# q rows read three half groups late, two short-lived PSUM tiles, a longer ring: one change to a sparse attention layer

## The chip, the cores and the metric

The kernel runs on one core of a Trainium2 chip. The metric is the device time of one execution in microseconds. The engines are named as the profile names them: PE is TensorE (PEld its weight loads), DVE is VectorE, ACT is ScalarE, POOL is GpSimd, SP is SyncE. Each engine runs its own queue of instructions in a fixed order. The order is fixed when the program is built, and an instruction that has to wait holds up everything behind it in its queue.

## The reference, cut to what matters

One layer of graph attention over 4096 nodes with 512 features and 8 heads of 64. A node attends only where the adjacency matrix has an edge. The matrix is sparse: a node has about 17 edges on average, itself included, and none has more than 39 here.

```python
hs = layer_norm(x, ln1_scale, ln1_bias)            # sources
ht = layer_norm(h_target, ln1_scale, ln1_bias)     # targets
q = (ht @ Wq + bq).reshape(T, H, HD) / sqrt(HD)
k = (hs @ Wk + bk).reshape(S, H, HD)
v = (hs @ Wv + bv).reshape(S, H, HD)
logits = einsum('thd,shd->hts', q, k)
probs = softmax(where(adj != 0, logits, NEG))
ctx = einsum('hts,shd->thd', probs, v).reshape(T, D)
ht = layer_norm(ht + ctx @ Wo + bo, ln2_scale, ln2_bias)
y = ht + gelu(ht @ W1) @ W2                        # W1: 512 x 2048, W2: 2048 x 512
x = layernorm(x + y)
```

## The kernel before

The kernel never forms the 4096 x 4096 logits. It has three stages that overlap.

1. Keys and values of all nodes are computed and written to DRAM (`kvd`, one row of 1024 floats per node). Meanwhile the adjacency matrix is read, a list of neighbours is made for each node (`edges`), and the nodes are sorted by degree (`sort`). This is done in two parts of 2048 nodes, A and B. The lists of B are made while attention on A already runs.
2. Attention works on tiles of 128 targets of similar degree. A tile has room for `cap` edges per target, between 11 and 39. The edges are taken in groups of S = 3: for each edge GpSimd gathers one row of `kvd` per target into a slot of a ring.
3. The feed-forward part (`feed`) runs on TensorE between the attention steps, one or two tiles behind.

For one group of edges, attention does this (cut; "..." marks what is left out):

```python
nc.vector.tensor_tensor(kv[:, :n, :D], kv[:, :n, :D], tq[:, :D]..., ALU.mult)    # L1169: k * q
nc.vector.tensor_reduce(lg[:, :n, :], ..., AX.X, ALU.add)                         # L1173: logits
if j0 > 0:
    nc.scalar.activation(p[:, j0:j0 + n, :], lg[:, :n, :], AF.Exp)                # L1177
advance()                     # one step of every front and finish that is under way
yield cost * n
if pend:
    values(*pend.pop())       # the group before this one, see below
    issue(k + AHEAD)          # AHEAD = 4: gathers of the group four further on
advance()
if j0 == 0:
    p = ps.tile([P, MAXE, H], F32, name="p")                                      # in PSUM
    nc.scalar.activation(p[:, :n, :], lg[:, :n, :], AF.Exp)                       # L1187
if n == S:
    by_scalar(kv, lg)         # ScalarE scales the third edge's values, L1149 and L1152
```

The stretch between two calls of `advance` is a half group. `values` scales the values by `p` (VectorE, L1132); in part B it adds two of the three edges first (L1136). TensorE then adds them up, transposed, in PSUM (L1140):

```python
nc.vector.tensor_tensor(v4, v4, p..., ALU.mult)                                   # L1132
if m > 1 and i >= NA:
    nc.vector.tensor_add(kv[:, 0, D:], kv[:, 0, D:], kv[:, 1, D:])                # L1136
for j in slots:
    for c in range(KC):
        nc.tensor.matmul(cps[:, c, :], kv[:, j, ...], ident, is_transpose=True, ...)   # L1140
```

Two generators are stepped by `advance`: `front` makes the q rows of a tile before it starts, `finish` brings a tile to an end. Each `yield` is half a group.

```python
def front(i):
    tq = sp.tile([P, 2 * D], F32, name="tq", bufs=3)
    gather(t, h_target, rec[:, TGT:TGT + 1])
    yield
    nc.scalar.activation(t, t, AF.Identity, ...)                                  # L978
    yield
    pt = ps.tile([P, KC, P], F32, name="t")
    nc.tensor.transpose(pt[:, kc, :], ...)                                        # L982
    nc.scalar.activation(hT[:, kc, :], pt[:, kc, :], ...)                         # L985
    yield
    yield
    pq = ps.tile([P, D], F32, name="t")
    nc.tensor.matmul(pq, hT[:, kc, :], wq[:, kc, :], ...)                         # L991
    nc.vector.scalar_tensor_tensor(tq[:, :D], pq, HD ** -0.5, bqr, ...)           # L993: the q row
    tqs[i] = tq

def finish(i, p, cps, group, hs, mv):
    pm = sp.tile([P, MAXE, H], F32, name="pm", bufs=1)
    nc.vector.scalar_tensor_tensor(pm, rec, 0.0, p, op0=ALU.is_gt, op1=ALU.mult)  # L1037
    nc.vector.tensor_reduce(sums[:, i, :], pm..., AX.X, ALU.add)                  # L1040
    ...                                                                           # 1 / sum: ri
    nc.scalar.copy(rxf..., ri...)                                                 # L1047
    yield
    yield
    prx = ps.tile([P, KC, P], F32, name="t")
    nc.tensor.transpose(prx[:, c, :], rxf..., ident)                              # L1053
    ct = sp.tile([P, KC, P], F32, name="rb", bufs=1)
    nc.scalar.copy(ct, prx)                                                       # L1055
    yield
    nc.vector.tensor_mul(ct, cps, ct)                                             # L1057
    yield
    yield
    pa = ps.tile([P, D], F32, name="t")
    nc.tensor.matmul(pa[:, c * P:(c + 1) * P], tq..., ident, is_transpose=True)   # L1063
    nc.tensor.matmul(pa, ct[:, c, :], wo[:, c, :], ...)                           # L1067
    yield
    h = sp.tile([P, D], F32, name="h")
    nc.scalar.copy(h, pa)                                                         # L1071
    ...                                              # layer norm of h, ending in L1084
    pt = ps.tile([P, 2, 2 * P], F32, name="t")
    nc.tensor.transpose(pt..., h..., ident)                                       # L1093
    nc.scalar.activation(h2T[:, kc, :w], pt[:, k, :w], ...)                       # L1097
```

The pool `ps` has one buffer for each name unless it says otherwise. So every tile named `t`, whether `pt`, `pq`, `prx` or `pa`, takes the same PSUM bank, and a new one waits until the one before it has been read. `cps` has two banks and `p` one; four more belong to the projections, and later to the feed-forward: `pf` (L1277, emptied by the Gelu at L1280) and `po` (L1286).

The gathered rows lie in a ring of RING = 17 slots, `place` gives each group its slots. The adjacency blocks and masks that the lists of part B need have buffers of their own (`a`, two of 4 KB per partition; `sg`, three of 1 KB). At the end `verdict` sets a flag, which all engines load into a register. It decides whether a general path that takes any adjacency matrix has to run as well; with these inputs it does not.

Of the kernel before, what the change touches and what calls it, by code (L numbers as in the profile page):

```python
# [8 lines left out]
F32 = mybir.dt.float32  # L9
# [8 lines left out]
P = 128  # L18
# [425 lines left out]
def adj_resnorm_kernel(  # L444
# [59 lines left out]
    RING = 17  # L504
# [10 lines left out]
    flag = const.tile([1, 1], I32, name="flag")  # L515

# [13 lines left out]
    with tc.tile_pool(name="keep", bufs=1) as keep:  # L530
# [17 lines left out]
        with ExitStack() as late:  # L548
# [13 lines left out]

            ring = kp.tile([P, RING, 2 * D], F32, name="kv")

# [31 lines left out]
            def list_constants():  # L596
                io = lp.tile([P, QW], I32, name="a", bufs=2)
# [4 lines left out]
                io = lp.tile([P, QW], I32, name="a", bufs=2)  # L602
# [18 lines left out]
            pc = ps.tile([P, D], F32, name="t")  # L621
# [73 lines left out]
            def quarter(i, h):  # L695
                if i < NA + FILL:
                    a = ring[:, (i * NQ + h) % DEEP, :].bitcast(I32)
                else:
                    a = lp.tile([P, QW], I32, name="a", bufs=2)
                nc.sync.dma_start(a, adj[i * P:(i + 1) * P, h * QW:(h + 1) * QW])  # L700
                return a

            def edges(i):
# [4 lines left out]
                for h in range(NQ):  # L708
# [5 lines left out]
                    sg = lp.tile([P, QW], U8, name="sg", bufs=3)  # L714
# [13 lines left out]
                dec = lp.tile([P, 2, SEG, 8], U16, name="dec")  # L728
# [65 lines left out]
            def sort(part):  # L794
# [6 lines left out]
                dif = pool.tile([P, n], F32, name="dif")  # L801
# [5 lines left out]
                b16 = pool.tile([P, n], BF16, name="b16")  # L807
                nc.vector.tensor_scalar(b16, dif, -1.0, float(NB - 1), op0=ALU.mult, op1=ALU.add)
                if part:
                    oh = pool.tile([P, QW], I32, name="a", bufs=2).bitcast(BF16)  # L810
# [6 lines left out]
                pos = pool.tile([P, QW], I32, name="a", bufs=2).bitcast(F32)  # L817
# [4 lines left out]
                for c in range(2):  # L822
                    sl = slice(c * w, (c + 1) * w)
                    pt = ps.tile([P, w], F32, name="t")
# [5 lines left out]
                for c in range(2):  # L830
                    sl = slice(c * w, (c + 1) * w)
                    pa = ps.tile([P, w], F32, name="t")
# [3 lines left out]
                rank = pool.tile([P, n], F32, name="rank")  # L836
                nc.vector.tensor_reduce(rank, pos.rearrange("p b i -> p i b"), AX.X, ALU.add)
                ranki = pool.tile([P, n], I32, name="ranki")
# [14 lines left out]
            def project(order, t=None):  # L853
# [28 lines left out]
                def turn(n):  # L882
# [4 lines left out]
                    for k2 in range(KC // 2):  # L887
                        pt = (psi if k2 else ps).tile([P, 2, GR], F32, name="pt" if k2 else "t")
# [80 lines left out]
            def front(i):  # L969
# [10 lines left out]
                pt = ps.tile([P, KC, P], F32, name="t")  # L980
# [8 lines left out]
                pq = ps.tile([P, D], F32, name="t")  # L989
                for kc in range(KC):  # L990
                    nc.tensor.matmul(pq, hT[:, kc, :], wq[:, kc, :], start=kc == 0,  # L991
                                     stop=kc == KC - 1)
                nc.vector.scalar_tensor_tensor(tq[:, :D], pq, HD ** -0.5, bqr,  # L993
# [8 lines left out]
            for _, _, n in SG:  # L1002
                if place[-1] + n > RING:
                    place[-1] = 0
                place.append(place[-1] + n)

# [4 lines left out]

            def issue(k):

                if k >= len(SG):
                    return
# [16 lines left out]
            def finish(i, p, cps, group, hs, mv):  # L1032
# [3 lines left out]
                pm = sp.tile([P, MAXE, H], F32, name="pm", bufs=1)  # L1036
                nc.vector.scalar_tensor_tensor(pm[:, :cap, :], rec[:, E0:E0 + cap].unsqueeze(2)  # L1037
                                               .to_broadcast([P, cap, H]), 0.0, p[:, :cap, :],
                                               op0=ALU.is_gt, op1=ALU.mult)
                nc.vector.tensor_reduce(sums[:, i, :], pm[:, :cap, :].rearrange("p j h -> p h j"),  # L1040
# [10 lines left out]
                prx = ps.tile([P, KC, P], F32, name="t")  # L1051
# [4 lines left out]
                yield  # L1056
                nc.vector.tensor_mul(ct, cps, ct)  # L1057
                yield
                yield
                pa = ps.tile([P, D], F32, name="t")  # L1060
# [28 lines left out]
                for k2 in range(KC // 2):  # L1089
                    pt = ps.tile([P, 2, 2 * P], F32, name="t")  # L1090
# [24 lines left out]
            def attention():  # L1115
# [38 lines left out]
                for k in range(AHEAD + 1):  # L1154
                    issue(k)
                yield 0.0
                k = 0
                for group in GROUPS:
# [3 lines left out]
                    for i in group:  # L1162
                        cps = ps.tile([P, KC, P], F32, name="cps", bufs=2)
                        while k < len(SG) and SG[k][0] == i:
# [15 lines left out]
                            if pend:  # L1180
                                values(*pend.pop())
                                issue(k + AHEAD)
                            advance()
                            if j0 == 0:

                                p = ps.tile([P, MAXE, H], F32, name="p")
# [14 lines left out]
            def verdict():  # L1201

                sf = sums.rearrange("p t h -> p (t h)")
                both = sp.tile([P, MAXE, H], F32, name="pm", bufs=1).rearrange("p j h -> p (j h)")
# [16 lines left out]
                pb = ps.tile([1, 1], F32, name="t")  # L1221
                nc.tensor.matmul(pb, b1, ones_bf[:, 0:1], start=True, stop=True)
                nc.vector.tensor_scalar(flag, pb, 0.5, None, op0=ALU.is_gt)
# [99 lines left out]


# [110 lines left out]
```

## Time and profile before

| what | value |
|---|---|
| time, median of 3 | 1874.77 us |
| span of the profiled execution | 1873.0 us |
| mean granted clock of TensorE | 0.963 |
| ACT_TABLE_LOAD before Gelu (L1280) | 110, 141.1 us |
| ACT_TABLE_LOAD before Exp (L1177, L1187, L1149) | 67, 22 and 20 |
| gathers of `kvd` rows (L952, POOL) | 603, 690.1 us |

In a row of the waits, the engine and line on the left stood idle until the engine and line on the right was done; then come the total in us, how many times, and the longest. In a row of groups come line, engine, operation, what it writes and reads, shapes and count; then busy time and mean ns of one, and the idle time ahead of it. A wait is put down to the releaser that came last. If the releaser belongs to other work than the waiter, it is a buffer that is waited for rather than a value.

### The profile page before, as it was taken

What the parts mean: (1) busy time and instruction counts of PE and PEld (TensorE: products, weight loads), DVE (VectorE), ACT (ScalarE), POOL (GpSimd) and SP (SyncE); (2) the same over time, 40 slices, a digit from 0 to 9 for tenths busy, and PEclk for the clock granted to TensorE, in tenths of its full rate; (3) what the DMA queues carried; (4) which work ended last, traced back from release to release, by engine and by line L of the source; (5) the groups of instructions that cost most, each with busy time, mean ns of one, the idle gap of its engine ahead of it and who ended that gap; (6) DMA issues with size and microseconds to landing.
All of it is one profiled execution on the core that took longest, in us unless ns stands there. A gap on an engine that the chain in (4) does not pass through costs nothing. (4 is left out here: it accounts for less than half of the span.)

```text
span 1873.0 us, 22926 instructions
## 1 busy us (share of the span) xinstructions
PE 1699.6 (91%) x7030; PEld 1097.4 (59%) x7030; DVE 1430.0 (76%) x2595; ACT 1242.5 (66%) x3133; POOL 881.9 (47%) x804
## 2 busy tenths in 40 slices
PE   7989884698998989999999989999999999999996
PEld 3444332466655656766666656566666566666664
DVE  6999855989998838677878889889877778788400
ACT  5777634577886737776777767777777677777411
POOL 1000143744545474656666666656555545554101
PEclk9999977898999999999999989999999999999998
DMA  9999949978877556777778778767676767766000
GB/s 348 375 373 377 348 154 341 330 269 300 306 276 252 203 170 213 262 242 258 260 248 283 276 268 279 267 229 251 225 240 227 259 219 236 238 222 222 23 1 24
DMA packets 147757, 463.28 MB, mean 247 GB/s; under 512 B 24468, under 2 KB 29160, under 8 KB 147624
## 3 DMA queue, kind: packets, MB, share of 16 engines
q0 software_dynamic: 95696, 342.19, 53.9%
q1 hardware_dynamic: 44112, 96.44, 14.5%
q10 hardware_dynamic: 7816, 23.08, 3.2%
q8 instruction: 58, 0.95, 0.2%
q14 instruction: 75, 0.61, 0.1%
HBM read 430.76 MB, written 30.89 MB: 246 GB/s over the span
## 5 line engine op out<-in xcount | busy, mean ns | idle before, releaser
L952 POOL DMA_INDIRECT kv<-kvd,rec x603 | 690.1, 1144 | 499.2 <-PE cps L1140 232.9
L1277 PE MATMUL pf<-h2T,w 128*128 128x256 f32 (+1 forms) x2176 | 475.6, 371 | 1.2 <-ACT h2T L1097 1.2
L1286 PE MATMUL po<-w,gt 128*128 128x512 f32 x1024 | 470.6, 601 | 3.3 <-ACT gt L1280 3.3
L1169 DVE TENSOR_TENSOR kv<-kv,tq 128x1536 f32<-128x1536 f32 (+2 forms) x211 | 352.5, 1676 | 108.9 <-DMA kv<-kvd,rec 97.8
L1277 PEld LDWEIGHTS pf<-h2T,w 128*128 128x128 f32 x2176 | 391.6, 193 | 65.8 <-issue 19.8
L1152 ACT ACTIVATE kv<-kv,pa 128x64 f32<-128x64 f32 x1520 | 391.5, 336 | 3.6
L1173 DVE TENSOR_REDUCE lg<-kv 128x24 f32<-128x1536 f32 (+2 forms) x211 | 350.7, 1668 | 1.7 <-ACT pa L1149 0.2
L1140 PE MATMUL cps<-ident,kv 128*128 128x128 f32 x2008 | 264.5, 279 | 54.2 <-DVE kv L1132 40.3
L1140 PEld LDWEIGHTS cps<-ident,kv 128*128 128x128 f32 x2008 | 238.0, 144 | 128.9 <-issue 49.2
L1286 PEld LDWEIGHTS po<-w,gt 128*128 128x128 f32 x1024 | 188.6, 193 | 193.8 <-issue 189.4
L1132 DVE TENSOR_TENSOR kv<-kv,p 128x1024 f32<-128x1024 f32 (+1 forms) x211 | 249.5, 1189 | 53.5 <-ACT p L1177 53.5
L674 POOL TENSOR_TENSOR n_rs<-n_ve,mhalf 128x2 f32<-128x2 f32 (+2 forms) x51 | 47.1, 924 | 335.2 <-DVE n_ve L667 150.9
L1280 ACT ACT_TABLE_LOAD x110 | 141.1, 1283 | 1.7
L917 PE MATMUL pq<-wk,h2T 128*128 128x512 f32 x256 | 125.3, 634 | 15.8 <-ACT h2T L902 8.1
L722 DVE MAX8 cand<-sg 128x8 uint16<-128x103 uint16 (+1 forms) x640 | 131.9, 251 | 0.5
L991 PE MATMUL t<-wq,tq 128*128 128x512 f32 x256 | 118.5, 606 | 10.8 <-ACT tq L985 8.0
L715 ACT ACTIVATE sg<-kv 128x1024 uint8<-128x1024 int32 x84 | 88.7, 1058 | 56.8 <-DMA kv<-in_adj_dram 23.4
L1280 ACT ACTIVATE gt<-pf 128x512 f32<-128x512 f32 x128 | 76.4, 597 | 75.0 <-PE pf L1277 73.9
L1067 PE MATMUL t<-wo,rb 128*128 128x512 f32 x256 | 119.2, 610 | 3.6 <-DVE rb L1057 3.6
L917 PE MATMUL pq<-wv,h2T 128*128 128x512 f32 x256 | 116.7, 598 | 1.3 <-ACT tq L919 1.3
L917 PEld LDWEIGHTS pq<-wk,h2T 128*128 128x128 f32 x256 | 49.8, 202 | 81.9 <-issue 51.4
L1177 ACT ACT_TABLE_LOAD x67 | 86.0, 1283 | 9.2 <-DVE lg L1173 7.4
(157 smaller groups left out, 1544.4 us busy)
## 6 DMA issues: line engine op xcount, KB each, us to landing
kv<-in_adj_dram SPq DMA_DIRECT2D x84, 512.0 KB, 7.5
a<-in_adj_dram SPq DMA_DIRECT2D x44, 512.0 KB, 6.4
kvd<-tq ACTq DMA_DIRECT2D x24, 512.0 KB, 6.6
kv<-kvd,rec POOLq DMA_INDIRECT x603, 5.7
kv<-in_L_gnn_h_target_dram SPq DMA_DIRECT2D x32, 256.0 KB, 7.7
kv<-in_x_dram SPq DMA_DIRECT2D x15, 512.0 KB, 8.9
rest_d<-gid SPq DMA_DIRECT2D x32, 160.0 KB, 5.0
w<-in_L_gnn_W_dram SPq DMA_DIRECT2D x4, 1024.0 KB, 9.5
```

What stands on the lines that cost most here:

```text
L722: nc.vector.max(cand[:, h * SQ + s, :], wd[:, w0:w1])
L917: nc.tensor.matmul(pkv, hT[:, kc, j * P:(j + 1) * P], w[:, kc, :], start=kc == 0, stop=kc == KC - 1)
L952: nc.gpsimd.indirect_dma_start(out=dst, out_offset=None, in_=table[:, :], in_offset=bass.IndirectOffsetOnAxis(ap=idx, axis=0))
L1067: nc.tensor.matmul(pa, ct[:, c, :], wo[:, c, :], start=False, stop=c == KC - 1, skip_group_check=True)
L1132: nc.vector.tensor_tensor(v4, v4, p[:, j0:j0 + m, :].unsqueeze(3) .to_broadcast([P, m, H, HD]), ALU.mult)
L1140: nc.tensor.matmul(cps[:, c, :], kv[:, j, D + c * P:D + (c + 1) * P], ident, is_transpose=True, start=j0 + j == 0 and c == 0, stop=j0 + n ...
L1152: nc.scalar.mul(v, v, pa[:, hd:hd + 1])
L1169: nc.vector.tensor_tensor(kv[:, :n, :D], kv[:, :n, :D], tq[:, :D].unsqueeze(1).to_broadcast([P, n, D]), ALU.mult)
L1173: nc.vector.tensor_reduce(lg[:, :n, :], kv[:, :n, :D].rearrange("p j (h d) -> p j h d", h=H), AX.X, ALU.add)
L1277: nc.tensor.matmul(pf[:, k, :], w1[(f0 + k) // KC][:, kc, (f0 + k) % KC * P:((f0 + k) % KC + 1) * P], h2T[:, kc, :w], start=kc == 0, stop= ...
L1280: nc.scalar.activation(gt, pf, AF.Gelu_apprx_tanh)
L1286: nc.tensor.matmul(po[j], gt[:, k, j * P:(j + 1) * P], w2[(f0 + k) // KC][:, (f0 + k) % KC, :], start=False, stop=f0 + k == FC - 1, skip_g ...
```

## The change

There are four parts. They share the aim of letting TensorE and VectorE wait less for each other and for gathers.

The first reads the q row off PSUM three half groups after TensorE has been asked for it, so that VectorE's queue does not stop there. It moves the steps of `finish` to suit.

```diff
@@ front
                     nc.tensor.matmul(pq, hT[:, kc, :], wq[:, kc, :], start=kc == 0,
                                      stop=kc == KC - 1)
+                yield
+                yield
+                yield
                 nc.vector.scalar_tensor_tensor(tq[:, :D], pq, HD ** -0.5, bqr,
@@ finish
                 nc.scalar.copy(ct, prx)
                 yield
+                yield
                 nc.vector.tensor_mul(ct, cps, ct)
                 yield
                 yield
-                pa = ps.tile([P, D], F32, name="t")
+                yield
+                yield
+                pa = ps.tile([P, D], F32, name="t", bufs=2)
```

The second gives the name `t` two PSUM banks everywhere. The bank comes from `p`, which moves to SBUF; the masked copy `pm` is no longer needed, since the mask is applied in place.

```diff
-                pt = ps.tile([P, KC, P], F32, name="t")
+                pt = ps.tile([P, KC, P], F32, name="t", bufs=2)
...                                            (the same at every other tile "t")
-                                p = ps.tile([P, MAXE, H], F32, name="p")
+                                p = sp.tile([P, MAXE, H], F32, name="p", bufs=1)
...
-                pm = sp.tile([P, MAXE, H], F32, name="pm", bufs=1)
-                nc.vector.scalar_tensor_tensor(pm[:, :cap, :], rec[:, E0:E0 + cap].unsqueeze(2)
+                nc.vector.scalar_tensor_tensor(p[:, :cap, :], rec[:, E0:E0 + cap].unsqueeze(2)
                                                .to_broadcast([P, cap, H]), 0.0, p[:, :cap, :],
```

The third gives the ring 20 slots in part B. They are the slots that the lists have used until then: `a`, `sg` and some small tiles of the lists become slices of slots 17 to 19. In part B the gathers are requested one group earlier.

```diff
-    RING = 17
+    RING = (17, 20)
...
-            ring = kp.tile([P, RING, 2 * D], F32, name="kv")
+            ring = kp.tile([P, RING[1], 2 * D], F32, name="kv")
+            wide = [ring[:, 17 + i, :].bitcast(I32) for i in range(2)]
+            tools = ring[:, 19, :]
+            signs = [tools[:, i * QW // 4:(i + 1) * QW // 4].bitcast(U8) for i in range(3)]
...
+            def request(k):
+                ahead = AHEAD + (1 if k >= first_b else 0)
+                while issued[0] <= min(k + ahead, len(SG) - 1):
+                    issue(issued[0])
+                    ...
+                    issued[0] += 1
...
-                                issue(k + AHEAD)
+                                request(k)
```

The fourth writes the flag only after the last output row has been scaled, so that no engine loads it, and branches on it, before the work is done.

```diff
-                nc.vector.tensor_scalar(flag, pb, 0.5, None, op0=ALU.is_gt)
+                nc.vector.tensor_scalar(raised, pb, 0.5, None, op0=ALU.is_gt)
...
                 if g + 1 == len(GROUPS):
                     while ends:
                         wind_up()
+
+                    nc.vector.scalar_tensor_tensor(flag, raised, xs[-1][0:1, 0:1], raised,
+                                                   op0=ALU.bypass, op1=ALU.max)
```

## The prediction

> **What bounds the kernel now.** I read the page first (busy shares, the clock row), then a table of stages, then the waits of TensorE and of VectorE inside the stages, then the clock around TensorE's longest gaps.
>
> ```profile
> PE 1699.6 (91%) x7030; PEld 1097.4 (59%) x7030; DVE 1430.0 (76%) x2595; ACT 1242.5 (66%) x3133; POOL 881.9 (47%) x804
> PEclk9999977898999999999999989999999999999998
> ```
>
> TensorE is busiest by far, and its clock row dips below 9 only in a few slices. By stages (columns: stretch, length, busy time of PE, PEld, DVE, ACT, POOL, then granted clock, DMA share, GB/s):
>
> ```profile
> 0.00:326.00 326.00, 267.22 (x689) 122.47 (x689) 251.03 (x1049) 197.43 (x375) 58.81 (x73) 0.93 0.91 330
> 326.00:640.00 314.00, 273.12 (x1267) 189.54 (x1268) 291.03 (x566) 229.87 (x611) 157.22 (x140) 0.93 0.80 279
> 700.00:1030.00 330.00, 316.35 (x1494) 220.70 (x1493) 258.54 (x258) 241.34 (x653) 202.41 (x176) 0.99 0.75 253
> 1030.00:1745.00 715.00, 681.76 (x2881) 455.14 (x2880) 589.38 (x624) 522.45 (x1387) 409.36 (x363) 0.98 0.72 240
> 1745.00:1855.00 110.00, 109.31 (x469) 73.58 (x468) 11.02 (x65) 23.02 (x41) 8.95 (x10) 1.00 0.05 18
> ```
>
> Up to 326 us the projections run beside the loading of the adjacency (DMA share 0.91); the change touches nothing that sets this stage. From 326 to 640 attention of part A runs beside the lists of part B: VectorE is busy 291 of 314 us, so it and TensorE share the bound. From 700 on TensorE is 95 to 96% busy. From 1745 to 1855 it alone finishes the feed-forward matmuls, 99% busy at full clock: whatever TensorE is late by in the middle ends up in the end time. So the change is worth what it removes of two things between 326 and 1745 us: TensorE's gaps, and half-clock time that follows them.
>
> The gaps of TensorE by releaser, first in 326 to 640, then in 1030 to 1745 (waiter, releaser, total us, times, longest):
>
> ```profile
> PE t L982 <- ACT rb L1055: 7.0, 2, 6.3
> PE t L1063 <- ACT tq L985: 7.0, 2, 5.5
> PE t L1093 <- ACT h2T L1097: 1.3, 2, 0.8
> ```
>
> ```profile
> PE cps L1140 <- DVE kv L1136: 13.9, 6, 5.0
> PE t L982 <- ACT h L1071: 3.6, 2, 3.3
> PE t L1063 <- ACT tq L985: 3.0, 2, 1.6
> PE t L982 <- ACT rb L1055: 2.4, 1, 2.4
> PE t L991 <- ACT h L1071: 2.0, 1, 2.0
> ```
>
> The reader is to see that most of these are not waits for an input. L982 transposes a q tile; `rb` (L1055) and `h` (L1071) belong to another tile. They stand there because both use the one PSUM tile `t`, which ScalarE has not emptied. The first row of the second fence is another kind: TensorE waits for values that VectorE has not scaled. VectorE in the same stretch:
>
> ```profile
> DVE tq L993 <- PE t L991: 37.4, 10, 6.8
> DVE kv L1169 <- DMA kv<-kvd,rec: 37.2, 20, 6.8
> DVE kv L1132 <- ACT p L1177: 29.5, 22, 4.1
> ```
>
> Every long gap is paid twice, as the clock shows around three of them (gaps at 417, 1089 and 1204 us):
>
> ```profile
> 415.00:430.00 15.00, 8.66 (x43) 6.92 (x41) 10.19 (x23) 6.97 (x23) 7.71 (x7) 0.77 1.01 378
> 1085.00:1100.00 15.00, 10.00 (x35) 6.67 (x35) 14.08 (x12) 11.46 (x36) 10.82 (x9) 0.77 0.85 290
> 1203.00:1215.00 12.00, 8.47 (x20) 4.37 (x19) 10.95 (x12) 6.66 (x23) 7.78 (x6) 0.72 0.82 282
> ```
>
> A clock of 0.77 over 15 us is 3.4 us lost beside the gap itself.
>
> **What the Trainium skill says.** "Perfetto Trace Analysis", section Matmuls (under Optimizing Tensor Performance): independent matmul groups should rotate through different PSUM banks, so that emptying one overlaps the next group. The trace agrees that one bank does not do this: the 417 us gap (6.33 us) ends when ScalarE, itself held 4.2 us by an adjacency load, copies `rb` out. "TensorE: Matmul & The Clock Gate", section What's actually happening: the clock drops to half after about 3.4 us without enough work and returns after as much sustained work. The 3.4 us losses above are what a 6.8 us stretch at half clock costs, so the trace agrees; it also shows that a gap of 2.45 us (at 1252) is followed by a clock of 0.83 over 10 us, so gaps shorter than 3.4 us count here. "ScalarE: Activation LUTs", section What ACT_TABLE_LOAD costs: 1283 ns for each switch of table set, plus a drain. The trace has 1283 ns in every such row.
>
> **The change part by part.**
>
> *Two tiles `t`.* The logits `p` move to SBUF, which frees the bank. No row gets longer: scaling 128x1024 from PSUM took 1.21 us and the product of the same size from SBUF alone took 1.22. The gaps that are waits for the bank are, by stage: 326 to 640: 7.0 + 7.0 + 1.3 + 0.3 = 15.6 us; 640 to 1030: 1.6 + 0.9 + 0.7 = 3.2; 1030 to 1745: 3.6 + 3.0 + 2.4 + 2.0 + 1.5 + 1.2 + 0.3 = 14.0. The half-clock time behind the longest (417, 599, 1252, 1479 us) cost 3.4 + 3.4 + 1.7 + 1.7 = 10.2 us: for each, window length times one minus clock. In the first stage VectorE is 93% busy and hands the gain on only in part: I choose 40% of 15.6 + 6.8, 9 us. Later TensorE is the bound: 80% of 17.2 + 3.4, 16.5 us.
>
> *Ring of 20, one request further ahead in part B.* The six waits `cps <- L1136` (13.9 us) lie at 1054 to 1207 us. In each, VectorE had itself just waited for a gather (2.3 us at 1084, 3.1 at 1128, 4.4 at 1198), and GpSimd had issued it late because its slots were held. A group takes 715 us / 105, 6.8 us, so one group of lead covers all of them. With half clock behind them (1.7 + 3.4 + 1.7 + 3.4) 24.1 us; I take 70%, 17 us.
>
> *q rows read three half groups later.* It removes up to 80.0 us of VectorE's waits (23 over the whole span; 37.4 in the stretch above). But while TensorE is the bound, VectorE waits because it is ahead, so I book nothing for this beside what the two parts above already hold. The order of the built programs agrees: in both, the q row still stands directly ahead of the next tile's two first products in most places. It also holds one `t` for three half groups. Counting steps for tiles of 4 to 13 groups, at most one other `t` is wanted meanwhile, since the output product moves by three half groups: no new wait is built in.
>
> *Extra steps in the finish.* They remove the waits of L1067 for `rb` (2.7 + 0.9, 3 us). They also put off the feed-forward: in TensorE's built order it starts after 120 value transposes where it started after 100, and up to the 600th there are 7 us less matmul work ahead (a 128x512 fp32 product counted 0.86 us as in the last stage). These 7 us are done later, where TensorE is full; half was idle time anyway, so I choose 5 us lost.
>
> *Table loads.* ScalarE's built order has 198 instead of 220: 22 x 1.283 = 28 us less on an engine that is not the bound. It shortens the path from logits to values; I book 3 us.
>
> *Late flag.* The flag is written after the last row is scaled (1858.1 us). Loading it took 0.5 us and the engines' branches were done 2.5 us later, while GpSimd's own loading stood at 1858.2 anyway: 0.5 us lost.
>
> *Sum.* -9 - 16.5 - 17 - 3 - 3 + 5 + 0.5 = -43. Since every order of TensorE's queue is new, some waits come at new places; I take 5 us for that: -38, and 1875 - 38 = 1837 us.
>
> **The rivals.** (1) The waits move. The queue orders are fixed ahead of time, so where ScalarE is late TensorE stops at its next instruction that needs it, whichever it is. For it: the gaps are 11 kinds, none over 32 us. Then only half of the 43 comes: 1852. (2) VectorE's 80 us are on the path and the whole middle runs faster: for it, 37.2 us of gather waits go as well, and VectorE is 93% busy up to 640. The ceiling is all gaps from 326 to 1745 (lengths less PE busy in the stages, 96 us with 640 to 700) and the half clock (length times one minus clock, 41 us); half of that gives 1806. Against it: 95% busy TensorE after 700. (3) The `t` held by q becomes the wait that replaces the old one: two places instead of one, but one blocked for about 10 us at 32 tiles. If only a third of the tiles lose 3 us, the gain is nearly gone, 1868. Against it: the count of steps above.
>
> **Range and chances.** From (2) weakened to (3): 1812 to 1864. The 2% mark is 1837.3, on my number: faster 0.48, within 0.47, slower 0.05.
>
> **What would show it.** TensorE's waits on `t` released by ScalarE rows of another tile fall from 33 us to under 8; `cps <- L1136` under 5; granted clock after 326 near 0.98; 198 table loads; VectorE's gather waits in part B halved; its q waits much smaller than 80 us without an equal gain in time; the last stage about 5 us longer. I am wrong if TensorE's gaps keep their sum under new names, or if rows wait for the q row's VectorE step.

## The result and the profile after

| | before | after |
|---|---|---|
| median | 1876.01 us | 1859.12 us (1855.24 to 1861.36) |
| ratio, 95% interval | | 0.9905 [0.9879, 0.9931] |
| profiled span | 1873.0 us | 1853.5 us |
| table loads | 220 | 198 |

The change makes the kernel 17 us faster. 38 us were forecast.

First the page of the kernel after (busy time and share of each engine; granted clock in 40 slices), then its table of stages (stretch, length, busy time of PE, PEld, DVE, ACT, POOL, then granted clock, DMA share, GB/s).

```profile
PE 1687.4 (91%) x7030; PEld 1102.1 (59%) x7030; DVE 1429.6 (77%) x2596; ACT 1214.4 (66%) x3111; POOL 962.7 (52%) x804
PEclk9999986799999999999999999899999999999998
```

```profile
0.00:326.00 326.00, 270.45 (x713) 127.99 (x713) 256.14 (x1045) 199.12 (x381) 63.10 (x77) 0.92 0.91 336
326.00:640.00 314.00, 272.79 (x1287) 190.50 (x1286) 294.71 (x580) 236.78 (x625) 180.06 (x142) 0.94 0.80 283
700.00:1030.00 330.00, 319.90 (x1500) 223.77 (x1499) 266.05 (x265) 240.61 (x667) 215.71 (x184) 0.99 0.78 266
1030.00:1745.00 715.00, 683.34 (x2921) 463.38 (x2920) 579.38 (x658) 497.50 (x1346) 449.77 (x352) 0.98 0.69 231
```

TensorE's share is what it was, and TensorE is idle 41.2 us in the second row and 31.7 in the fourth, against 40.9 and 33.2 before. ScalarE has 28 us less to do, GpSimd 81 us more. Then the waits of TensorE, first in 326 to 640 us, then in 1030 to 1745 (waiter, releaser, total us, times, longest):

```profile
PE cps L1169 <- DVE kv L1161: 16.1, 9, 4.0
PE t L1079 <- ACT rb L1073: 10.1, 2, 6.7
PE t L1079 <- ACT h2T L1126: 8.1, 2, 7.0
PE t L994 <- ACT tq L990: 4.3, 1, 4.3
```

```profile
PE t L994 <- ACT tq L990: 14.8, 3, 9.5
PE t L1079 <- ACT h2T L1126: 5.7, 2, 5.4
PE t L1003 <- ACT tq L997: 5.7, 3, 2.1
PE t L1122 <- issue: 3.4, 2, 3.0
PE cps L1169 <- DVE kv L1165: 1.4, 1, 1.4
```

The last row was 13.9 us before: it is gone. So are the rows in which a q tile's transposition waited for `rb` or `h` of another tile. In their place TensorE waits for ScalarE's scaling of a gathered q tile (L990, which was L978). At L1079, which was L1053, it waits 8.1 + 5.7 us for `t` again, until ScalarE has emptied another tile's (L1126). The sum of TensorE's gaps after the first transposition of values (`cps`) is 92.5 us. It was 95.3.

Where did 19.5 us of span go? TensorE's matmuls from that first transposition to the end add up to 1382.2 us in every kernel, counting each at its full pace (429, 215 and 109.5 ns for 512, 256 and 128 columns). What lies above it is idle time and half clock; call it the loss. With the start and the end it makes up the span:

| us | before | after | difference | forecast |
|---|---|---|---|---|
| first transposition of values | 326.6 | 318.5 | -8.1 | 0 |
| loss in attention and feed-forward | 144.9 | 132.0 | -12.9 | -38.5 |
| from the start of the last matmul to the end | 19.3 | 20.8 | +1.5 | +0.5 |

The forecast column is the prediction's sum without its flag term. So a third of the forecast came where it was booked, and 8 us came in the stage that the prediction said the change does not touch. These are single executions; the two profiled ones took 1.3 and 3.9 us less than the medians of their kernels.

### The profile page after: what moved, and what is told of

Same layout as the page of the kernel before. It is cut to its first block, busy times and chain, and to the rows that moved or that the text cites. A ratio compares the mean times of both kernels' runs of the same rounds, so it can differ in the third digit from the quotient of the medians.

```text
span 1853.5 us, 22978 instructions
## 1 busy us (share of the span) xinstructions
PE 1687.4 (91%) x7030; PEld 1102.1 (59%) x7030; DVE 1429.6 (77%) x2596; ACT 1214.4 (66%) x3111; POOL 962.7 (52%) x804
## 5 line engine op out<-in xcount | busy, mean ns | idle before, releaser
L964 POOL DMA_INDIRECT kv<-kvd,rec x603 | 751.4, 1246 | 396.5 <-PE cps L1169 150.0
L1304 PE MATMUL pf<-h2T,w 128*128 128x256 f32 (+1 forms) x2176 | 470.7, 370 | 0.0
L687 POOL TENSOR_TENSOR n_rs<-n_ve,mhalf 128x2 f32<-128x2 f32 (+2 forms) x51 | 51.4, 1008 | 354.2 <-DVE n_ve L680 167.9
L728 ACT ACTIVATE kv<-kv 128x1024 uint8<-128x1024 int32 x128 | 134.9, 1055 | 73.2 <-DMA kv<-in_adj_dram 44.5
L1205 ACT ACTIVATE p<-lg 128x24 f32<-128x24 f32 (+2 forms) x179 | 39.3, 220 | 139.3 <-DVE lg L1201 114.4
L735 DVE MAX8 cand<-kv 128x8 uint16<-128x103 uint16 (+1 forms) x640 | 129.9, 252 | 0.5
L1003 PE MATMUL t<-wq,tq 128*128 128x512 f32 x256 | 118.7, 606 | 10.2 <-ACT tq L997 9.5
L990 ACT ACTIVATE tq<-tq,rec 128x512 f32<-128x512 f32 x32 | 26.1, 815 | 107.0 <-DMA tq<-in_L_gnn_h_target_dram,rec 91.9
```

The source lines that it names most:

```text
L728: nc.scalar.activation(sg, a, AF.Sign, accum_out=dpart[:, i, h:h + 1])
L735: nc.vector.max(cand[:, h * SQ + s, :], wd[:, w0:w1])
L964: nc.gpsimd.indirect_dma_start(out=dst, out_offset=None, in_=table[:, :], in_offset=bass.IndirectOffsetOnAxis(ap=idx, axis=0))
L1304: nc.tensor.matmul(pf[:, k, :], w1[(f0 + k) // KC][:, kc, (f0 + k) % KC * P:((f0 + k) % KC + 1) * P], h2T[:, kc, :w], start=kc == 0, stop= ...
```

## The experiments

Two theories stood against each other at first, and each expectation below says what they mean for its run. Roughly, theory 1: the parts are worth what their waits measured, but one of them hides a cost. Theory 2: queues have fixed orders, so a removed wait is followed by another where ScalarE or a gather is late. From the shift of ScalarE's scaling on they are sharpened: theory A says that ScalarE's wait for the q row's gather is the wait that took over; theory B, that any wait does. All ratios are to the kernel before, on the same chip in the same runs.

### The parts, one at a time

Ring and earlier request taken back:

```diff
-    RING = (17, 20)
+    RING = (17, 17)
-                ahead = AHEAD + (1 if k >= first_b else 0)
+                ahead = AHEAD
```

> The changed kernel, with the ring held at 17 slots and the requests at four groups ahead in part B too. Theory 1 (the extra lead is eaten: in part B the changed kernel's gathers take 1305 ns to issue instead of 1137, 104 us instead of 58 above the 945 ns of an undisturbed one, and the q rows' own gather stands behind them): the time stays within 5 us of the changed kernel's 1859, and the gathers go back to about 1140 ns. Theory 2 (the ring works as predicted and the shortfall lies with the PSUM tiles): 15 to 25 us slower than the changed kernel, 1874 to 1884, with waits of the value transposes for L1165 back at 10 us or more.

Measured: 1865.59 us, 0.9951 [0.9933, 0.9968].

The kernel before with only the two tiles `t`, the logits `p` moved to SBUF for it:

```diff
-                pt = ps.tile([P, KC, P], F32, name="t")
+                pt = ps.tile([P, KC, P], F32, name="t", bufs=2)
...                                  (every tile "t", p and pm as in the change)
```

> The kernel before with two PSUM tiles t alone, p in SBUF. Theory 1: this part works roughly as predicted, 15 to 25 us faster than before, 1851 to 1861. Theory 2 (the waits for t move to other releasers, since ScalarE's queue is late as a whole and not with one tile): under 8 us, 1868 to 1876, with the sum of TensorE's gaps from 326 to 1745 us within 10 us of the 96 of before.

Measured: 1865.30 us, 0.9942 [0.9925, 0.996].

The six extra steps (three ahead of the q row's VectorE step, three in the finish) taken back:

```diff
-                yield
-                yield
-                yield
                 nc.vector.scalar_tensor_tensor(tq[:, :D], pq, ...)
...                                  (and three in finish)
```

> The changed kernel with the six extra steps taken out: the q row is read at once as before, and the finish has its old steps. If the late reading works on the path (rival 2 of the prediction), 10 us or more slower than the changed kernel, 1869 or more. If the steps cost what the prediction booked (5 us lost, 3 us won) it is within 4 us, 1855 to 1863. If they are what ate the gain, 8 us or more faster, 1851 or less.

Measured: 1869.30 us, 0.9969 [0.9951, 0.9987].

The flag as before:

```diff
-                nc.vector.tensor_scalar(raised, pb, 0.5, None, op0=ALU.is_gt)
+                nc.vector.tensor_scalar(flag, pb, 0.5, None, op0=ALU.is_gt)
...                                  (without the late write)
```

> The changed kernel with the flag written where it was before. As predicted: within 1.5 us of the changed kernel. If the late flag delays the end by the branches' instruction fetch: 3 us or more faster, and the stretch from TensorE's last matmul to the end of the span is shorter by as much (it was 18.7 us before and 20.2 after).

Measured: 1856.00 us, 0.9895 [0.9851, 0.9939].

The two tiles give 10.9 us (7.5 to 14 by the interval) against 25.5 booked. The ring gives 0.46%, 8.6 us, against 17; without it a gather of `kvd` rows still takes 1225 ns in the mean (1246 with it, 1144 before), so the ring is not what made the gathers longer. The ring without the steps gives nothing on top of the two tiles (0.9969 after 0.9942), nor do the steps without the ring (0.9951): a gain shows only with both. With the steps taken back the time is what the expectation names for a late reading that works on the path (rival 2); what else it can be is seen below. The late flag shows in its place: from the start of the last matmul to the end 20.8 us with it, 19.5 without. The time is 3.1 us lower without it, which is within the intervals.

What the two tiles did is seen in the waits of TensorE from 326 to 1745 us, in the kernel that has nothing else:

```profile
PE t L992 <- ACT tq L986: 31.4, 9, 5.9
PE cps L1140 <- DVE kv L1132: 21.5, 8, 6.5
PE po L1286 <- ACT gt L1280: 12.4, 3, 10.4
PE t L1093 <- ACT h L1084: 12.3, 4, 5.9
PE t L1067 <- DVE rb L1057: 11.6, 5, 4.9
```

No row is left in which a q tile waits for another tile's `t`. But the q product (L992) now waits 31.4 us for ScalarE's eviction of the same tile, where it waited 6.1 before (`PE t L991 <- ACT tq L985: 6.1, 5, 2.1`): TensorE has got past one instruction and stops at the next that needs ScalarE. The loss is 142.0 us, against 144.9. More than half of what this profile gains lies ahead of attention, where the first transposition comes at 322.1 us instead of 326.6. What is different there is the list of part A. It takes two products with ones and then two with a triangle (`lower`) through `t`, and VectorE reads each. First the kernel before, then the changed kernel (durations in ns, then first and last start in us):

```profile
L825 PE MATMUL t<-oh,ones_bf x2: 322/400/478, 227.3 to 234.8; 128*128 128x384 bf16 x2
L833 PE MATMUL t<-oh,lower x2: 326/425/524, 238.5 to 241.5; 128*128 128x384 bf16 x2
```

```profile
L838 PE MATMUL t<-oh,ones_bf x2: 322/324/326, 225.0 to 226.1; 128*128 128x384 bf16 x2
L846 PE MATMUL t<-oh,lower x2: 479/503/527, 234.1 to 236.0; 128*128 128x384 bf16 x2
```

TensorE is not the one that gains. It stands 5.5 us ahead of the second product before, and 5.4 and 5.9 us ahead of the third with two tiles alone and in the changed kernel, each time until VectorE comes to its first scan. The bank wait has moved by one product here as well. But behind that scan the list needs fewer turns between the two engines. From the start of the scan to the first scatter of records by GpSimd, which needs the ranks, it takes 7.9 to 8.0 us in the fifteen profiles with two `t` and 10.3 to 11.8 in the five with one. The last projections follow, since ScalarE, which copies them out, stands until the records have landed (before, then two tiles alone):

```profile
268.10 0.58 ACT L919 COPY kv<-pq 128x512 f32<-128x512 f32 x1 [12.36 <-DMA rec<-R,ranki]
```

```profile
264.75 0.59 ACT L920 COPY kv<-pq 128x512 f32<-128x512 f32 x1 [10.51 <-DMA rec<-R,ranki]
```

The last projection starts at 292.1 us before and at 287.3 with two tiles alone. The first transposition comes at 326.6 to 333.8 us in the five kernels with one `t` (mean 329.8) and at 315.2 to 323.4 in the fifteen with two (mean 319.6).

### How much a mere order is worth

One constant delays the list work of part B in the build. It changes only the interleaving of the queues, and with it the number of table loads (210 and 196 instead of 198 in the two shifts of the changed kernel, 212 instead of 220 in that of the kernel before).

```diff
-            WAIT = 40.0
+            WAIT = 44.0
```

> The changed kernel with one constant of the build changed, by which the lists of part B start later among the other work (40 to 44); no instruction is added or removed, only the order of the queues is another. If an order is as good as another, it is within 3 us of the changed kernel. If the particular order carries a large part of the gain (theory 3: single parts cannot be weighed closer than what a chance order gives), it differs by 5 us or more, either way.

Measured: 1880.13 us, 1.0026 [1.0006, 1.0046]: 21 us slower than the changed kernel.

The same in the kernel before:

> The same constant changed in the kernel before. As with the changed kernel: within 3 us of before if the order does not matter, 5 us or more away if it does.

Measured: 1889.23 us, 1.0082 [1.0029, 1.0135]: 14 us slower.

And 36 instead of 40 in the changed kernel:

> The changed kernel with the one constant that delays the second part's list work at 36 instead of 40 (44 cost 21 us). It removes and adds no work; only the interleaving of the queues moves. Theory B: 1850 to 1885 us, off by 5 us or more in one direction, with the excess on TensorE off by as much and no root in common. Theory A says nothing of its size; an unchanged time (within 4 us) would say that 44 was a special case and that order scatter is small.

Measured: 1877.85 us, 1.0013 [1.0002, 1.0024]: 19 us slower.

A new order alone moves these kernels by as much as the whole change does. Both shifts were for the worse, so 40 looks chosen for orders near these. A single part of 5 to 10 us can't be weighed by one build, and neither can the 12 us of the steps.

### Is ScalarE too full?

The Gelu is left out (ReLU stands in its place), so that the switches of table sets go, 281 us of them in the kernel before, and ScalarE has that much more room:

```diff
-                    nc.scalar.activation(gt, pf, AF.Gelu_apprx_tanh)
+                    nc.scalar.activation(gt, pf, AF.Relu)
```

On the kernel before:

> The kernel before with ReLU in place of the Gelu (the Gelu is left out), so that ScalarE never changes its table: 219 loads, 281 us of ScalarE's time, are gone. Theory 1 in its wider form (TensorE's gaps are ScalarE's queue being late, and a second bank only moves the place where TensorE meets it): TensorE's excess over its matmul work falls from 112 us to 85 or less and the time to 1845 or less. Rival (the gaps come from gathers and from VectorE): time above 1862, excess above 100 us.

Measured: 1879.37 us, 1.0024 [1.0008, 1.004].

On the changed kernel:

> The changed kernel with ReLU in place of the Gelu. Theory 1: with ScalarE relieved, the second bank and the ring bring what was predicted of them, and the changed kernel with ReLU is 25 us or more faster than the one of before with ReLU. Rival: the difference stays at the 17 us measured with the Gelu, or is smaller, since the bank was a limit only where ScalarE was late.

Measured: 1861.98 us, 0.993 [0.9904, 0.9955].

A fifth of ScalarE's work goes and no time with it, in either kernel, and the pair stays 17.4 us apart (16.9 with the Gelu). Unless a worse order hid the gain both times, ScalarE is late, but not because it is busy. What it does instead is to be seen at the changed kernel's longest gap, in the timelines of TensorE, ScalarE and GpSimd there (start, length, engine, line, operation; in brackets the idle time before it and its releaser):

```profile
1180.34 1.04 PE L1169 MATMUL cps<-ident,kv 128*128 128x128 f32 x8
1190.90 1.11 PE L994 MATMUL t<-ident,tq 128*128 128x128 f32 x4 [9.53 <-ACT tq L990]
```

```profile
1180.87 0.22 ACT L1205 ACTIVATE p<-lg 128x24 f32<-128x24 f32 x1
1190.03 0.81 ACT L990 ACTIVATE tq<-tq,rec 128x512 f32<-128x512 f32 x1 [8.94 <-DMA tq<-in_L_gnn_h_target_dram,rec]
```

```profile
1179.45 3.99 POOL L964 DMA_INDIRECT kv<-kvd,rec  x1 [0.30 <-issue]
1183.75 0.95 POOL L964 DMA_INDIRECT xt<-in_x_dram,rec  x1 [0.30 <-issue]
1185.01 1.29 POOL L1281 DMA_INDIRECT out_dram<-xt,rec  x1 [0.30 <-issue]
1186.60 0.97 POOL L964 DMA_INDIRECT tq<-in_L_gnn_h_target_dram,rec  x1 [0.30 <-issue]
```

TensorE waits 9.53 us for ScalarE, ScalarE 8.94 us for the gather of the q rows. GpSimd starts that gather only at 1186.60, behind others in its queue, one of which took 3.99 us. ScalarE's queue holds everything behind it meanwhile. In the whole changed kernel ScalarE stands 104 us ahead of this one line from 300 us on, in the kernel before 78 us; 89.7 and 66.6 us of that end when the gather has landed. With the Gelu left out in the kernel before it is 88.5 us.

### Moving the wait by steps of the build

ScalarE's scaling is put one half group later in part A and two in part B:

```diff
                 gather(t, h_target, rec[:, TGT:TGT + 1])
                 yield
+                yield
+                if i >= NA:
+                    yield
                 m = rec[:, RST:RST + 2].bitcast(F32)
                 nc.scalar.activation(t, t, AF.Identity, bias=m[:, 1:2], scale=m[:, 0:1])
...                                  (one step less ahead of the product in part A)
```

> The changed kernel, with ScalarE's scaling of a gathered q tile put one half group later in the first part (one of the two half groups ahead of the product goes for it) and two later in the second part (where there is room for it); nothing else. Following every TensorE gap above 0.8 us back through its releasers, 28 us of the changed kernel's gaps end at a q row's gather that ScalarE waits for (9 us before), and 30 us at a gather of keys and values (46 us before). Theory A (the wait moved: the deeper ring took 16 us off the key-value gathers and the q row's gather, issued late from GpSimd's queue, put 19 us in their place): ScalarE's 90 us of waits for the q gather fall below 30 us, the gaps that end at it below 8 us, their sum with the half clock falls by 20 us or more, and the time is 1825 to 1842 us, ratio 0.973 to 0.982. Theory B (whichever wait is taken away, the order fixed at build leaves about 100 us of excess, and other roots take over): ScalarE's waits fall as well, but the excess stays at 95 to 115 us and the time at 1850 to 1875 us, ratio 0.987 to 1.0.

Measured: 1853.71 us, 0.9888 [0.9868, 0.9908].

On the changed kernel with the early flag:

> The same shift of ScalarE's scaling, on the changed kernel with the flag written as before (1856 us, ratio 0.990). Theory A: 1822 to 1840 us, ratio 0.971 to 0.981, with q-gather roots from 36 us to under 8. Theory B: 1848 to 1875 us, in either direction from the run without the shift, and not the same step as the shift makes in the changed kernel itself.

Measured: 1853.28 us, 0.9884 [0.9864, 0.9903].

On the kernel before, two half groups:

> The kernel before, with ScalarE's scaling of a gathered q tile and all that follows it two half groups later in both parts (the tile is needed three half groups after its product as it stands, one after with the shift); nothing else. In this kernel only 9 us of TensorE's gaps end at a q gather. Theory A: 1862 to 1872 us, ratio 0.993 to 0.998, a small gain, because the root is small here. Theory B: a new order as good as any other, 1860 to 1890 us, with no relation to the 9 us.

Measured: 1877.86 us, 1.0009 [0.9998, 1.0019].

The times are those of theory B, but they decide nothing, since ScalarE's wait for the gather, which both theories expected to fall, did not. ScalarE's waits from 326 to 1745 us, shifted kernel first, changed kernel second:

```profile
ACT tq L993 <- DMA tq<-in_L_gnn_h_target_dram,rec: 117.2, 28, 10.2
```

```profile
ACT tq L990 <- DMA tq<-in_L_gnn_h_target_dram,rec: 89.7, 21, 12.5
```

In the other two it is 119.1 us against 103.7 with the early flag alone, and 88.7 against 66.6 in the kernel before. The scaling follows the issue of its gather by 5.2 us in the median, and by 4.9 in the changed kernel. In ScalarE's queue its place hardly moves. The number of exponentials of `p` ahead of it, for eight tiles of part B:

```
changed kernel   133 136 145 149 158 162 171 175
shifted          133 136 144 149 157 162 170 174
```

A step of the generator only says which instruction is offered first. It seems that the build places the scaling by a time of its own for the gather, and that the gather lands later than that; no run shows it.

### Moving it by a dependency

So the scaling was made to depend on something later. It reads its mean and deviation from a small tile that VectorE makes from the record plus zero times a logit of the group that was just reduced:

```diff
                 gather(t, h_target, rec[:, TGT:TGT + 1])
                 yield
+                yield
+                yield
                 m = rec[:, RST:RST + 2].bitcast(F32)
+                if latest:
+                    nc.vector.scalar_tensor_tensor(tied, latest[-1][:, 0, 0:2], 0.0, m,
+                                                   op0=ALU.mult, op1=ALU.add)
+                    m = tied
                 nc.scalar.activation(t, t, AF.Identity, bias=m[:, 1:2], scale=m[:, 0:1])
...                                  (the product and the q step close up in part A)
```

> The changed kernel with ScalarE's scaling of a gathered q tile really later: the scaling now reads its mean and deviation from a tile of two columns that VectorE makes after the logits of the next group (its record times one, plus zero times a logit), so that the build can't put it ahead of them; one small VectorE instruction a tile more, 29 in all, and the product and VectorE's q step close up in the first part. The shift by yields alone left the scaling 5.2 us behind its gather and ScalarE waited 119 us for it. Theory A (ScalarE's wait for the q gather is a root that costs about 28 us): ScalarE's waits for the q gather fall below 30 us, TensorE's gaps that go back to it below 10 us, the excess below 85 us, and the time is 1828 to 1844 us. Theory B (other roots take over whatever wait is removed): ScalarE's waits fall, TensorE's gaps move to another name, the excess stays at 95 to 115 us, the time at 1850 to 1880 us.

Measured: 1826.85 us (1825.09 to 1830.72), 0.9733 [0.9707, 0.9759].

> The kernel before with the same tie, and its chain of q rows two half groups later. Theory A: its q roots are 9 us, so 1862 to 1872 us. Theory B: 1865 to 1890 us, with the gaps under other names.

Measured: 1846.51 us, 0.9829 [0.9801, 0.9856].

> The same tie on the changed kernel with the flag written as before (1856 us without the tie, q roots 36 us, excess 99 us). Theory A: 1824 to 1840 us. Theory B: 1848 to 1880 us.

Measured: 1825.28 us, 0.9724 [0.9697, 0.9751], the fastest of all.

The q rows' gather taken off GpSimd. The rows that meet are then other ones, so what is left out is the gathering itself:

```diff
-                gather(t, h_target, rec[:, TGT:TGT + 1])
+                nc.sync.dma_start(t, h_target[i * P:(i + 1) * P, :])
```

> The changed kernel with the q rows' gather left out of GpSimd's queue: SyncE loads 128 consecutive rows of the same size in its place, so that the rows that meet are other ones; 32 of 602 gathers less on GpSimd, and nothing else changed. Theory A: no TensorE gap goes back to a q gather (28 us in the changed kernel), and the time falls by 20 us or more, to 1825 to 1840 us. Theory B: the gaps go back to key-value gathers and VectorE instead, the excess stays at 95 to 115 us, the time within 15 us of 1859.

Measured: 1833.54 us, 0.9768 [0.9739, 0.9797].

In the tied changed kernel the scaling follows its gather by 21.4 us in the median. ScalarE's waits for it, then TensorE's largest waits, both from 326 to 1745 us:

```profile
ACT tq L999 <- DMA tq<-in_L_gnn_h_target_dram,rec: 10.2, 3, 4.7
```

```profile
PE cps L1180 <- DVE kv L1172: 18.0, 7, 4.6
PE cps L1180 <- issue: 7.1, 2, 3.9
PE t L1133 <- ACT h L1124: 6.4, 5, 2.5
PE t L1013 <- ACT tq L1006: 6.1, 4, 2.1
```

89.7 us have become 10.2, TensorE's gaps 61.4 us instead of 92.5, and the loss 104.9 instead of 132.0. No other wait of TensorE took over. VectorE's wait for the q product even doubled, from 34.0 to 67.7 us, and cost nothing. Theory B is refuted for this wait: it is a cause, worth 32 us in these kernels, while the wait of VectorE and the load of ScalarE gave nothing when they fell. That the time falls by 26 us where the gather is off GpSimd agrees, though it is no clean removal: ScalarE still waits 39.9 us for the loaded rows there. The tie also makes a new order; but the three mere orders above were all slower, and the three tied kernels are all about 32 us faster.

Theory A is half right. The size of the wait is as it said, but the change did not bring it: the kernel before gains 32 us as well, where 3 to 13 us were expected. Following each gap of TensorE back to the first transfer had shown only 9 us for it in the kernel before, so that account is too small where several waits hang together. And the tied pair stands to one another as the untied pair does: 0.9733 over 0.9829 is 0.990 (about 0.004 either way), against 0.9905. So the q wait hid nothing of the change's gain.

### The parts once more, with the wait gone

The tied kernel before, with the two tiles `t` alone:

> The kernel before with the tie (1846.5 us, ratio 0.983) and of the change only the two t tiles and the logits in SBUF. With ScalarE's wait for the q gather gone, what is left of the bank waits should be seen undisturbed. If the two tiles are worth what I booked (26 us, most of it on TensorE's gaps), 1821 us; if they are worth what they gave without the tie (10.9 us), 1836; if their gain was a matter of order alone, 1841 to 1850. The changed kernel with the tie took 1826.9.

Measured: 1831.58 us, 0.9777 [0.9755, 0.9799].

The tied changed kernel without the ring, the q chain closed up in part B too:

> The changed kernel with the tie (1826.9 us) and a ring of 17 slots with no request further ahead in the second part; the q chain closes up there as it does in the first part. If the ring is worth what I booked (17 us), 1844 us; if it is worth what leaving it out cost without the tie (6.5 to 9 us), 1833 to 1836; if nothing, 1827.

Measured: 1857.76 us, 0.9915 [0.9887, 0.9942].

The two tiles give 0.52%, 10 us by the ratios, as without the tie. The rest of the change adds 0.44%, 8 us. The account by stretches for the first:

| us | tied before | with two `t` | changed, tied |
|---|---|---|---|
| first transposition of values | 333.8 | 318.6 | 317.7 |
| loss in attention and feed-forward | 109.9 | 109.8 | 104.9 |

In attention the two tiles are worth 3 us in one pair and nothing in the other (144.9 to 142.0, and 109.9 to 109.8); the rest of their gain is ahead of it. The last run is no clean answer on the ring, since the q chain had to be squeezed for it. It is 31 us slower than the tied changed kernel (34 by the ratios), and of the tie's 32 us it keeps only about 7 (0.9915, and 0.9951 for the untied kernel without the ring), although ScalarE's wait for the q gather is down there too, from 112.2 to 5.6 us. So removing that wait does not pay everywhere. TensorE then waits for ScalarE's eviction ahead of its q product, in the tied kernel without the ring and, unsqueezed, in the untied one:

```profile
PE t L1011 <- ACT tq L1006: 20.5, 9, 5.7
```

```profile
PE t L1003 <- ACT tq L997: 26.7, 8, 5.8
```

With the ring it is 6.1 us tied and 9.5 untied. Since the wait is there with and without the squeeze, the squeeze need not be its reason. How the 31 us divide between ring and squeeze is open.

## Why the prediction was off

The direction was right and the time lies in the range, but less than half of the 38 us came. By its own steps:

- **Two tiles `t`, -25.5 us: the step that failed.** With two tiles alone the waits that it counted vanished; in the changed kernel 15.0 us of the kind stand again, nearly all at L1079, where under 8 were forecast. But the step took a share (40 and 80%) of them, with the half clock behind them, as a saving, and in attention they were worth 0 to 3 us. TensorE waited there because ScalarE was late, and the bank only named the place. The prediction had seen this at 417 us, where ScalarE had itself stood 4.2 us for a transfer, and still booked the gap for the bank. With two banks TensorE stopped at the next one, the q product: from 6.1 to 31.4 us in the kernel with two tiles alone.
- **"The change touches nothing that sets this stage" (up to 326 us) was wrong.** The list of part A uses `t` too, and its ranks come 2.4 to 3.8 us sooner after VectorE's scan. By the means over all profiles the first transposition of values comes 10 us sooner with two tiles, about the whole of what they gave.
- **Ring, -17 us: mis-sized, and its sign came by luck.** `cps` behind VectorE's sum fell from 13.9 to 1.4 us as forecast. But it is 2.0 us with two tiles alone and 3.3 in the changed kernel without the ring, so it was not the ring that took it away. Of the three gathers that the prediction calls late because slots were held, only that at 1128 us follows such a hold (GpSimd stands 2.0 and 1.7 us for slots still being read). Ahead of 1084 GpSimd issues one after another with 0.3 us between, and ahead of 1198 it stood 3.0 us for an output row's transfer. The ring is worth 8.6 us (0.46%), with about 6 either way, and only with the steps. VectorE's gather waits in part B were to be halved; they went from 37.2 to 32.9 us.
- **q rows later, 0: right.** The q step has the same place among VectorE's products in 30 of 32 tiles. Its waits from 326 to 1745 us fell from 75.6 to 34.0, with no equal gain, and rose again to 67.7 with the tie, with no loss.
- **Steps of the finish -3, feed-forward later +5.** The last stage, from the last transposition of values to the last matmul, is 104.4 us instead of 97.5: +6.9. The steps as a whole, in the changed kernel, are worth 12 us (0.9969 to 0.9905), which is inside what an order alone can do.
- **Table loads, -3.** 22 are gone as counted. No gain of theirs is to be seen: 281 us of them off ScalarE gained nothing.
- **Late flag, +0.5.** 1.3 to 1.5 us at the end of the profile.
- **New orders, +5.** An order alone cost 14 to 21 us in three trials, so the term was too small, and the 80% range was none too wide.
- **Clock.** Near 0.98 as forecast from 700 us on; the 0.94 from 326 to 640 is as good as before.

The sign that the prediction named for being wrong is what happened: TensorE's gaps keep their sum (95.3 and 92.5 us) under new names. Rival (1), with 1852 us, was nearest. Rival (2) is refuted in its cause: VectorE's waits fell by half and little came of it, and doubled with the tie while the kernel got 32 us faster. Rival (3) did not come: the q row's hold on one `t` made no wait of its own (no gap of TensorE from 326 to 1745 us ends at L1008).

What the prediction had in hand and did not use was ScalarE's row for the q gather, 66.6 us in the kernel before:

```profile
ACT tq L978 <- DMA tq<-in_L_gnn_h_target_dram,rec: 66.6, 19, 14.2
```

It asked who released TensorE, and not what that releaser had been waiting for.

Not settled is why ring and steps need each other, why the tie gives 7 us and not 32 without the ring, and how the 12 us of the steps divide into less waiting and mere order.

## What to carry to other kernels

When a bank or a buffer is named as the releaser, ask what its holder was waiting for, and count the wait as a saving only if that one is on time. An engine with a fixed queue order that stops for a transfer holds everything behind it: put such an instruction behind a true dependency that is later than the transfer, because a hint to the builder did not move it here. Before weighing parts of some microseconds, measure what a mere reordering does.

## What was not expected of the hardware

GpSimd's gathers of `kvd` rows took 690.1 us before and 751.4 after, though their number is the same (603). It is not the ring: with 17 slots it is 738.4 us, and with two tiles `t` alone already 751.3. The five kernels with `p` in PSUM have 688.8 to 699.4 us, the fifteen with `p` in SBUF 738.0 to 770.3. So it comes with the move of `p` to SBUF and the second `t`, which no run has apart; what VectorE does meanwhile points to `p`. The mean duration of a gather by what VectorE does meanwhile (overlap above 0.3 us):

| kernel | `p` in | beside scaling of values by `p` | beside no such scaling | beside k * q |
|---|---|---|---|---|
| before | PSUM | 1252 ns (137) | 1113 ns (466) | 1609 ns (175) |
| two `t` alone | SBUF | 1582 ns (171) | 1113 ns (432) | 1699 ns (187) |
| after | SBUF | 1618 ns (168) | 1102 ns (435) | 1650 ns (207) |

The Trainium skill, "GPSIMD Engine Reference", section 1. Specifications, says that GpSimd's access to SBUF is shared with VectorE, and names VectorE instructions with two SBUF inputs as a case of contention. The trace agrees: k * q always had two, and the scaling has two since `p` moved; with `p` in PSUM a gather beside it was 0.33 us shorter. Beside neither of the two, a gather took 954 ns before and 957 after. The prediction looked at VectorE's own durations only, which did not change. What these 61 us of GpSimd cost the whole was not tried, since it takes a PSUM bank for `p` beside two for `t`.
